# Attention layer 1 in two passes over its pairs of heads, with landmarks as means of projected tokens and pinv beside attn1

## The chip, the cores and the metric

The kernel runs on one core of a Trainium2 chip. The core has five engines that run beside each other and meet at semaphores: TensorE (PE in the profile, its weight loads PEld), VectorE (DVE), ScalarE (ACT), GpSimd (POOL) and SyncE (SP), which here issues most DMAs. Matmul results land in PSUM, [...]; everything else lives in SBUF or in DRAM. The metric is the device time of one launch in microseconds, the median of several runs.

## The reference

The input is `x` of 2 x 512 x 64 x 32, that is two batches of 2048 tokens with 512 channels, all in fp32. Layer 0 is full softmax attention with 8 heads of 64 and an embedding added to queries and keys, an output projection and a residual. Layer 1 is Nyström attention on the layer-normed tokens, and then a feed-forward map that is one 512 x 512 matrix (a 4-bit table product with `W`), each with a residual. In short:

```
q, k, v = split(ln(t) @ Wqkv);  q = q * scale
qL, kL  = means of q and k over groups of l = 8 tokens       # 256 landmarks
attn1   = softmax(q @ kL.T)       # 2048 x 256
attn2   = softmax(qL @ kL.T)      # 256 x 256
attn3   = softmax(qL @ k.T)       # 256 x 2048
out = attn1 @ (pinv(attn2) @ (attn3 @ v)) + conv33(v)
t = t + out @ Wout + bout;   t = t + ln(t) @ M
```

`pinv` is six steps of an iteration with 256 x 256 products. Its start is scaled by the largest row and column sums over all heads and both batches, so no head's pseudo-inverse can start before `attn2` of every head is there. Because a mean commutes with a projection, the landmarks can be had either by projecting means of tokens or by taking means of projected tokens.

## The kernel before, in words

Heads are worked in pairs: 64 + 64 channels fill the 128 partitions, and there are 4 pairs in each of 2 batches, numbered n = 0 to 7. Tokens are taken in four blocks of 512 (`TB`, `NTB`).

TensorE, VectorE, ScalarE and GpSimd execute in exactly the order in which the Python code emits their instructions; SP's DMAs are placed by the framework as soon as their buffers allow. So the code is a set of generators ("units") that yield after a piece of work, and the order of the calls decides what stands beside what. `advance(gens, n)` runs up to n units; a generator can yield `GAP` to let one call pass.

Layer 0: `attention0(hd, filler, ...)` runs one pair's attention, 64 steps of scores, exp and values, and between them units of the next pair's projections (`Heads0.units`) or of a batch's end (`finish0_units`, which calls `norm0_steps` for the layer norm of layer 1 and writes the normed tokens `xn` to DRAM as `xh`). `norm0_steps` also sums `xn` over groups of 8 tokens (L992), which gives the pooled tokens.

Layer 1, landmarks: `Landmarks.project` (L1178) multiplies the pooled tokens with the weights of q and k (`lp`, L1183), `attend` makes `attn2` (`X`), and `gram` makes its Gram matrix (`A`). `landmarks_beside(0)` does so for batch 0 beside the last attention of layer 0; `landmarks_staged(1)` (L1268) does so for batch 1 in a stretch of its own before the first pair. `X`, `A` and the landmarks `L` go to DRAM. Then `start_scale` makes the common scale.

Layer 1, pairs: the loop at L1850 does for each n, one after the other: `attn3` with the pair's `queries` (L1399, L1366); `landmarks_values` (attn3 @ v, normed, `Y`); `convolution` into the output tile `o`; `iteration_start` (L1476: load `A`, scale it into `M`, multiply `X` with `Y`); `pinv` (L1533: five iterations of squares `pa` and `pb`, each followed on VectorE by `less`, L1552, and on ScalarE by `flip`, which copies a transposed block; then three products `wp`, `tp`); the next pair's `keys`; and `attn1` with the next pair's `values`. `attn1` (L1614) keeps its scores in a tile of two PSUM banks with one exp over both, its values in a bank of its own, and the sums `rs` in a bank `pp`, where a reciprocal on VectorE (L1642) reads them.

PSUM is full: two banks `pp`, taken in turn by every `bank(...)`; two tiles `sc` of two banks each; and `av0`, `av1`, taken in turn by `values_bank`.

The end of a batch, `finish1_units` (L1716), is for each token block the output projection `yp` (four units), a layer norm (`mean`, squares, `var`), and the map `fp` (four units, each of which reads the `fp` of the unit before). Batch 0's end is filler: three units at each of the ten places of `pinv` for n = 4, and what is left is drained at n = 5, at the line

```python
            while hp == 1 and fill:
                advance(fill)
```

Batch 1's end comes last, with its own order (`turns`).

## Time and profile before

| | us |
|---|---|
| median of 3 runs (lowest, highest) | 2877.85 (2871.69, 2879.75) |
| the profiled execution's own time | 2879.97 |
| its span, first to last instruction | 2878.2 |
| TensorE busy with matmuls | 2787.5 |
| VectorE busy | 1746.6 |
| ScalarE busy | 870.6 |
| GpSimd busy | 262.5 |
| layer 0 up to its last attention | 0 to 1275 |
| that attention, with batch 0's landmarks | 1275 to 1464 |
| batch 1's norm beside pair 0 | 1464 to 1581 |
| batch 1's landmarks | 1581 to 1644 |
| the pairs of layer 1 | 1644 to 2750 |
| the end of batch 1 | 2750 to 2878 |

A row of the groups gives the line, the engine, the operation, what it writes and reads, how often, and then busy time in us, the mean of one in ns, and idle time before it with what ended it. A matmul of the code in fp32 shows as two rows of the trace. Matmuls overlap, so the busy time of a group is less than its count times its mean; the time from one start to the next is what counts. In a stage table each line is a stretch: its limits, its length, busy time (and number of instructions) of PE, PEld, DVE, ACT and POOL, the granted TensorE clock, the DMA share and GB/s.

### The profile page before, as it was taken

How to read it: one execution, taken by the hardware profiler on the slowest of the kernel's cores; microseconds unless marked ns; L12 is line 12 of the kernel's file. 1: busy time of each engine (PE TensorE's matmuls, PEld its weight loads, DVE VectorE, ACT ScalarE, POOL GpSimd, SP SyncE). 2: the span in 40 equal slices, each digit the busy share in tenths (PEclk: the TensorE clock that was granted, in tenths of full speed). 3: DMA queues.
4: the chain of work that ended last, by engine and by line, in shares of the span. 5: the costliest groups of instructions: out<-in, count | busy, mean ns of one | idle time of the engine just before them, and what ended most of it. 6: DMA issues, size and time to landing. Idle time of an engine off the chain costs nothing. (4 is left out here: it accounts for less than half of the span.)

```text
span 2878.2 us, 39302 instructions
## 1 busy us (share of the span) xinstructions
PE 2787.5 (97%) x16834; PEld 1384.1 (48%) x16834; DVE 1746.6 (61%) x1955; ACT 870.6 (30%) x1158; POOL 262.5 (9%) x160
## 2 busy tenths in 40 slices
PE   8999999999999999999999999999999988999999
PEld 4343443434343343344444756566656534565633
DVE  3869788765667857657558364535445544454475
ACT  1344434433243344444331221212121301222110
POOL 1101011010101100100002010101010100001010
PEclk9999999999999999999999999999999999999999
DMA  3000000101012100022024200002000010000021
GB/s 114 1 5 1 5 1 1 60 15 45 27 47 73 51 1 1 1 79 79 28 74 167 87 14 17 17 20 83 6 23 32 17 53 34 10 19 13 1 72 47
DMA packets 78152, 103.59 MB, mean 36 GB/s; under 512 B 8320, under 2 KB 48016, under 8 KB 77712
## 3 DMA queue, kind: packets, MB, share of 16 engines
q1 hardware_dynamic: 73472, 84.16, 9.1%
q0 software_dynamic: 4416, 16.79, 1.5%
q8 instruction: 134, 2.20, 0.3%
q14 instruction: 50, 0.41, 0.0%
q10 hardware_dynamic: 80, 0.03, 0.0%
HBM read 64.13 MB, written 36.84 MB: 35 GB/s over the span
## 5 line engine op out<-in xcount | busy, mean ns | idle before, releaser
L1060 DVE TENSOR_TENSOR acc_f<-acc_f,p_f 128x1024 f32<-128x1024 f32 x448 | 609.9, 1361 | 239.6 <-ACT p_f L1050 211.3
L1050 ACT ACTIVATE p_f<-sc_f 128x1024 f32<-128x1024 f32 x512 | 497.0, 1022 | 574.0 <-PE sc_f L1042 566.5
L1042 PE MATMUL sc_f<-q_f,k_f 64*64 64x512 f32 x4096 | 494.2, 598 | 3.3 <-ACT p_f L1050 3.3
L1072 PE MATMUL av_f<-p_f,v_f 64*64 64x512 f32 x4096 | 484.0, 589 | 0.0
L1072 PEld LDWEIGHTS av_f<-p_f,v_f 64*64 64x64 f32 x4096 | 156.6, 133 | 282.9 <-issue 282.9
L1042 PEld LDWEIGHTS sc_f<-q_f,k_f 64*64 64x64 f32 x4096 | 144.2, 133 | 292.0 <-issue 251.6
L1329 PE MATMUL pp<-xh,w 128*128 128x512 f32 x512 | 234.2, 603 | 5.8 <-ACT q L1335 2.3
L1540 PE MATMUL pa<-M 128*128 128x192 f32 (+1 forms) x640 | 156.9, 381 | 0.0
L1645 POOL TENSOR_TENSOR o<-o,rinv 128x512 f32<-128x512 f32 x32 | 58.3, 1821 | 1028.2 <-DVE rinv L1643 1025.5
L1540 PE MATMUL pb<-R 128*128 128x192 f32 (+1 forms) x640 | 151.2, 379 | 0.0
L1329 PEld LDWEIGHTS pp<-xh,w 128*128 128x128 f32 x512 | 93.5, 191 | 117.4 <-issue 102.4
L1091 POOL TENSOR_TENSOR q_f<-q_f,rinv_f 128x512 f32<-128x512 f32 x32 | 67.5, 2109 | 850.1 <-DVE rinv_f L1090 850.1
L1642 DVE RECIPROCAL rinv<-rs 128x512 f32<-128x512 f32 x32 | 107.4, 3356 | 56.2 <-PE rs L1638 56.2
L909 PEld LDWEIGHTS vp<-w,xh 128*128 128x128 f32 x1024 | 118.4, 194 | 25.8 <-ACT p L1610 14.6
L909 PE MATMUL vp<-w,xh 128*128 128x128 f32 x1024 | 124.0, 280 | 3.3 <-ACT R L1516 3.3
L1540 PEld LDWEIGHTS pb<-R 128*128 128x128 f32 x640 | 113.9, 193 | 25.5 <-issue 0.5
L1540 PEld LDWEIGHTS pa<-M 128*128 128x128 f32 x640 | 111.5, 196 | 25.0 <-issue 2.0
L909 PEld LDWEIGHTS vp_f<-wv_f,x 128*128 128x128 f32 x1024 | 115.6, 192 | 12.7 <-issue 10.2
L924 PE MATMUL yp_f<-q_f,wo_f 128*128 128x512 f32 x256 | 118.8, 619 | 2.4 <-DVE rinv_f L1090 2.4
L864 PE MATMUL pp_q_f<-x,wq_f 128*128 128x512 f32 x256 | 118.4, 616 | 1.1 <-DVE ft_q_f L850 0.7
L909 PE MATMUL vp_f<-wv_f,x 128*128 128x128 f32 x1024 | 118.5, 276 | 0.0
L924 PE MATMUL yp_g<-o,wo_f 128*128 128x512 f32 x256 | 113.4, 596 | 4.0 <-DVE xb_g L931 2.2
(193 smaller groups left out, 2973.6 us busy)
## 6 DMA issues: line engine op xcount, KB each, us to landing
x<-in_x_dram SPq DMA_DIRECT2D x8, 1024.0 KB, 5.3
xr_f<-in_x_dram SPq DMA_DIRECT2D x8, 1024.0 KB, 5.0
x_fd<-xr_f POOLq DMA_DIRECT2D x8, 1024.0 KB, 4.7
xh_fd<-xn_f POOLq DMA_DIRECT2D x8, 1024.0 KB, 4.6
xh<-xh_fd SPq DMA_DIRECT2D x8, 1024.0 KB, 5.0
xb_g<-x_fd SPq DMA_DIRECT2D x32, 256.0 KB, 4.6
out_dram<-xb_g SPq DMA_DIRECT2D x32, 256.0 KB, 2.3
w<-in_wqkv_dram SPq DMA_DIRECT2D x24, 256.0 KB, 3.7
```

What stands on the lines that cost most here:

```text
L864: nc.tensor.matmul(pp, lhsT=w_sb[kind][:, k, cols], rhs=xbs[t][:, k, :], start=k == 0, stop=k == KC - 1)
L909: nc.tensor.matmul(vp[:, j * P : (j + 1) * P], lhsT=xb[:, k, j * P : (j + 1) * P], rhs=w_of(k), start=k == 0, stop=k == KC - 1,)
L924: nc.tensor.matmul(yp, lhsT=wo_sb[:, k, m * P : (m + 1) * P], rhs=oTs[k][:, toks], start=k == 0, stop=k == NPAIR - 1,)
L1042: nc.tensor.matmul(sc[r * D : (r + 1) * D, h, :], lhsT=hd.k[rows, lo : lo + D], rhs=hd.q[rows, t * TB : (t + 1) * TB], start=True, stop=True,)
L1050: nc.scalar.activation(p, sc, AF.Exp, scale=D**-0.5)
L1060: nc.vector.tensor_tensor(acc, first if c == 1 else acc, p, ALU.add)
L1072: nc.tensor.matmul(av[r][half, :], lhsT=hd.v[keys, c, half], rhs=pp[keys, h, :], start=c == 0, stop=c == NST - 1,)
L1091: nc.gpsimd.tensor_tensor(o, o, rinv, ALU.mult)
L1329: nc.tensor.matmul(pp, lhsT=self.w[:, k, j, :], rhs=self.xhs[t][:, k, :], start=k == 0, stop=k == KC - 1)
L1540: nc.tensor.matmul(dst, lhsT=lhsT[:, k, t * P : (t + 1) * P], rhs=rhs[:, k, :], start=k == 0, stop=k == 1)
L1642: nc.vector.reciprocal(rinv, rs)
L1645: nc.gpsimd.tensor_tensor(o, o, rinv, ALU.add)
```

## The change

Layer 1 is cut into two passes over all eight pairs.

Pass 1 does for each pair the projections, the landmarks, `attn2` with its Gram matrix, `attn3`, the product of `X` with `Y` (now stored as `y0`), and the convolution. `Pair.front` yields how many units of another generator go after each piece, and `beside` puts the next pair's projections (`keys`, `queries`, `values`) there. The landmarks come from the projected keys and queries: `landmarks_of` sums 8 tokens at a time on VectorE. Pooled tokens, `Landmarks.project`, `landmarks_beside` and `landmarks_staged` are gone. Queries `q`, outputs of the convolution `o`, `y0`, `A` and `L` go to DRAM.

Pass 2 does for each pair `load` (all of these back, a pair ahead), `iteration_start` (the scaling alone) and `pinv(slot)`. A slot runs one unit of the attn1 of the pair before, and one unit of `fill`: the last pair's convolution at n = 0, batch 0's end from n = 5 on. There is a slot before `pinv`, two in each of its five iterations, one before the last flip and two in each of the three products, 18 in all. After the last pair, its attn1 and what is left of `fill` run by turns.

`attn1` now takes single `pp` banks for its scores, with one exp for each head, and does its blocks one after the other; `pinv`'s flips and transposes use the bank `av0` alone, attn1's values `av1`.

```diff
-    def norm0_steps(b, t, xb, xn, part, pooled=None):
+    def norm0_steps(b, t, xb, xn, part):
...
-        other = nc.vector if t == NTB - 1 else nc.gpsimd
-        other.tensor_tensor(xn[:, 2:, :], xn[:, 2:, :], wide, ALU.mult)
+        nc.gpsimd.tensor_tensor(xn[:, 2:, :], xn[:, 2:, :], wide, ALU.mult)
...
-        for to, of in parts:
-            nc.vector.tensor_reduce(to, of.rearrange("p k (m l) -> p k m l", l=POOL), AX.X, ALU.add)
...
+        def landmarks_of(self, j, src, scale):
+            L = self.L[:, j, :]
+            nc.vector.tensor_reduce(L, src.rearrange("p (m l) -> p m l", l=POOL), AX.X, ALU.add)
+            nc.vector.tensor_scalar(L, L, scale / POOL, None, ALU.mult)
+            self.largest(2 + j, L)
+            self.largest(j, src)
...
+        def front(self, then=lambda: None):
+            self.attend()
+            yield 2
+            for h in range(2):
+                self.gram(h)
+                yield 0
+            then()
+            for _ in self.attn3():
+                yield 1
+            for _ in self.landmarks_values():
+                yield 1
+            for _ in self.start_values():
+                yield 1
...
+        def load(self):
+            self.A = [zpool.tile([P, 2, LM + 1], F32, tag=f"Q{h}", name=f"A_{self.name}_{h}") for h in range(2)]
...
+                    nc.sync.dma_start(self.A[h][:, t, cols], A_d[self.b, self.hp, h][:, t, cols])
...
+            nc.sync.dma_start(self.q, q_d[self.b, self.hp])
...
+            nc.sync.dma_start(self.o, o_d[self.b, self.hp])
...
-                advance(gens, n_fill)
+                slot()
                 for h in range(2):
                     pr = square(R[h], f"pb_{it}_{h}_{self.name}", flip)
                     less_in_blocks(M[h], rest, M[h], pr)
                     flip = None
-                advance(gens, n_fill)
+                slot()
                 self.flip(M[0], f"M0_{it}")
...
-                    sc = scores_bank(f"sc1_{self.name}_{t}_{j}")
-                    for h in range(2):
+                    scs = [bank(f"sc1_{self.name}_{t}_{j}_{h}") for h in range(2)]
+                    for h, sc in enumerate(scs):
...
+                    for h, sc in enumerate(scs):
+                        nc.scalar.activation(p[:, h, :], sc, AF.Exp, scale=D**-0.5)
                     yield
...
+    rest = chain(next_keys, pairs[1].queries(), pairs[1].values())
+    conv = pairs[0].convolution()
     for n, (b, hp) in enumerate(todo):
+        pair = pairs[n]
         if n:
+            for _ in beside(pair.front(start_scale if n + 1 == len(todo) else lambda: None), rest):
+                pass
+        drain(rest)
+        if n + 1 < len(todo):
+            for _ in pair.convolution() if n else conv:
+                pass
...
+    pairs[0].load()
+    ones_before, fill = [], [pairs[-1].convolution()]
+    def slot():
+        advance(ones_before)
+        advance(fill)
...
+    for n, (b, hp) in enumerate(todo):
+        pair = pairs[n]
+        if not n:
+            advance(fill, 2)
+        advance(ones_before, 2)
+        pair.iteration_start()
+        if n + 1 < len(todo):
+            pairs[n + 1].load()
+        slot()
+        pair.pinv(slot)
+        while ones_before:
+            advance(ones_before)
+        ones_before.append(pair.attn1())
+        os.append(pair.o)
+        if hp == 0 and b:
+            fill.append(finish1_units(b - 1, os[:NPAIR]))
+            os = os[NPAIR:]
+    while ones_before or fill:
+        advance(ones_before)
+        advance(fill)
```

## The prediction

> **What bounds the kernel now.** I read the busy table first, then groups of instructions by shape, then the stages, then single timelines.
>
> ```profile
> PE 2787.5 (97%) x16834; PEld 1384.1 (48%) x16834; DVE 1746.6 (61%) x1955; ACT 870.6 (30%) x1158; POOL 262.5 (9%) x160
> ...
> L1183 PE MATMUL lp<-pooled,wL 128*128 128x256 f32 x128 | 31.0, 399 | 1.2 <-ACT X L1209 1.2
> L1642 DVE RECIPROCAL rinv<-rs 128x512 f32<-128x512 f32 x32 | 107.4, 3356 | 56.2 <-PE rs L1638 56.2
> ```
>
> TensorE bounds it: what it no longer does is saved, what makes it wait is lost. A full 512-column row costs 0.43 us in a stream (32 `yp_f` in 13.83 us at 1481.72), so a matmul in the code, which is two rows, costs 0.86. Next, busy time by stage (length, then PE, PEld, DVE, ACT, POOL, clock):
>
> ```profile
> 1581.00:1644.00 63.00, 58.08 (x286) 44.96 (x284) 23.31 (x52) 16.47 (x39) 3.65 (x9) 0.95 0.33 107
> 1842.70:1973.30 130.60, 128.99 (x722) 79.53 (x720) 63.42 (x99) 30.34 (x55) 11.98 (x8) 1.00 0.06 17
> 2334.60:2415.00 80.40, 61.03 (x128) 25.63 (x127) 37.06 (x38) 6.84 (x9) 0.00 (x0) 0.85 0.13 44
> 2722.70:2750.00 27.30, 24.39 (x114) 8.53 (x112) 18.18 (x18) 9.63 (x13) 4.22 (x2) 1.00 0.21 71
> ```
>
> In order: batch 1's landmarks; one whole pair (n=2), nearly full at full clock; the part of batch 0's end that runs alone; the last pair's attn1. The slack is in stages 1 and 3. The timelines show why pinv needs no filler and where two PSUM banks bind:
>
> ```profile
> 1893.10 0.81 PE L1540 MATMUL pb<-R 128*128 128x192 f32 x4
> ...
> 1895.29 0.75 DVE L1553 SCALAR_TENSOR_TENSOR M<-M,pb 128x320 f32<-128x320 f32 x2 [0.57 <-PE pb L1540]
> ...
> 1896.81 0.27 PE L1530 MATMUL tp_M<-ident,M 128*128 128x128 f32 x1
> ...
> 2347.87 1.12 PE L946 MATMUL mean_g<-xn_g,mean_w 128*128 128x512 f32 x2 [2.83 <-DVE xn_g L943]
> 2355.12 2.05 PE L959 MATMUL var_g<-sq_g,mean_w 128*128 128x512 f32 x2 [6.13 <-DVE sq_g L956]
> ...
> 2746.55 3.35 DVE L1642 RECIPROCAL rinv<-rs 128x512 f32<-128x512 f32 x1
> ...
> 2749.95 3.70 PE L924 MATMUL yp_g<-o,wo_f 128*128 128x512 f32 x8 [1.51 <-DVE rinv L1642]
> ```
>
> One pinv iteration is 7.7 us with TensorE full: VectorE finishes head 0's `M` at 1896.04 and its flip comes at 1896.81. The last line is a matmul waiting until a 3.35 us reciprocal lets go of one of the two `pp` banks.
>
> [...] stage 3 reads 76% busy, but its 128 rows at 0.43 us are 55 of 80.4 us. [...] granted clock 0.85 in stage 3, 0.95 in stage 1, 1.00 where there are no gaps. [...]
>
> **The change, part by part** (us against the profiled execution: 2879.97, span 2878.2, 1.8 around it; the median 2877.85 is 0.35 below that span).
>
> (A) The `lp` matmuls go for both batches: 128 rows, 31.0 busy: **-30**. In their place `landmarks_of` reduces projected tokens on VectorE: 16 reduces of 128x2048 at the 2.29 us of `big<-k`, about 37, which the pass-1 stages hide (VectorE works half of a pair's time). Pooling leaves: 12 reduces, 18.5. No other matmul is added or lost; transposes and flips keep their number (two flips move from `iteration_start` into `pinv`).
>
> (B) Batch 1's landmark stage: at stream pace its work is 46.3 of 63.0 (`lp` 13.8, scores 3.4, gram 10.5, `pp` 6.9, `vp` 10.8, `wp_y` 0.9, each rows by 0.43 per 512 columns), so 16.7 is waiting. Afterwards `attend` and `gram` of pairs 1 to 6 have the next pair's projections beside them. Pair 7 has none: exp 0.60 (the 128x512 row of `X<-sc`), reduce 0.68, reciprocal 0.17, multiply 0.69 leave about 2.8 open; reciprocal 1.76, multiply 0.42 and three copies to `y0`, 3.4; the reload of `A`, whose buffer is the `X` just used, 2.1 to land plus issue and scaling, 2.5; half clock, 2: about 11. **-6**.
>
> (C) Without pooling, batch 0's last norm in layer 0 loses a 2.28 reduce before a `mean` that waited 2.84, and some half clock: -4; batch 1's norm beside pass 1 likewise -4 (its waits from 1524 on). **-8**.
>
> (D) Batch 0's end: before, 80.4 less 55 is about 26 of waiting. Afterwards its 40 units go one to a slot through pinv of n=5 to 7, 56 calls for 54 slots. A slot runs one attn1 unit (scores, scores, values, `rs` in turn) and then one of these, so I wrote both sequences side by side. In three slots, an `rs` falls beside a map unit whose predecessor `fp` still holds the other bank: `fp` waits for VectorE's tail 1.65 (head 1's `less`, from 1893.10 to 1894.71) and the reciprocal 3.35, less its own 0.96: 4 each, 12. In seven, scores (now two single banks) wait until VectorE has passed `less` and read `fp`: 1.6 each, 11. Mean beside `rs` (subtract 2.29 behind the reciprocal), squares 2.3 on ACT ahead of a flip's copy, sqrt with table loads: 9. `xr` has one buffer: after the last store (2.3) and reload (4.6) VectorE stands with pinv's `less` behind it, three times 2.3: 7. Switches: 5. Sum 44. **+18**.
>
> (E) The last attn1 has no fill left. With two banks a block takes 8.4: `rs` 0.96, reciprocal to 4.45, second score half, two exps of 0.60 each, values 1.8, `acc` 1.22. Four blocks: 5.4 + 3x8.4 = 30.6, against 21.1 before (19.0 from 2730.96, and two score units earlier). **+9.5**.
>
> (F) attn1 in the slots of the next pinv. Queued behind each `rs` reciprocal on VectorE are pinv's `less`: 1893.10 shifted by `rs` makes VectorE free at +5.7, so head 0's `M` is 0.5 late for its flip: 0.65 with the switch, three times. Score units put 1.2 of exp ahead of the flip's copy: 0.5, three times. The 16 attn1 units last only to slot 13 of 0 to 17; at n=1 to 4 the last two products have nothing beside them: copy and transpose 0.65 twice, and the last `rs` reciprocal stands before `less`: 3.1. A switch to a group that waits costs 0.1 to 0.26 beside its pace in stage 2 (8 `pp` rows take 3.63 for 3.43, 32 `vp` 3.77 for 3.51). Per pair then, pass 1: projections 8x0.2, values 4x0.26, attn3 1.4, gram 0.6, convolution 0.7, the rest 0.7, together 6.0. Pass 2: pinv's own 1.85 as before, `rs` 1.95, the three score units 1.5, the other units 1.4, the first two score units 1.0 (their banks are waited for), products 5.3 (3.1, two times 0.65, switches), together 13.0. That is 19.0, against 11.3 in stage 2 (130.6 less its work at pace, 119.3) plus 1.5 for landmarks: +6.2 for n=1 to 4, 25; n=5 to 7 have fill there, +2.8, 8; [...]. **+40**.
>
> (G) `landmarks_of` in the last layer-0 attention, 5.2 of VectorE at its end ahead of the residual adds: +4; n=0 without fill in its products: +1. **+5**. Moved DMAs: each pair stores `q`, `o` (1 MB, about 5 us like `xh`), `y0`, `A` and `L` in pass 1 and loads them in pass 2, all on SP; `X`, `pooled` and the landmarks' weights leave it. The 32 large ones are 160 us of 1500 and I put them at 0: they are issued a pair ahead, hidden by a pair's 68 to 75 us of other work. Without that cover each would cost its 5.
>
> Sum: -30 - 6 - 8 + 18 + 9.5 + 40 + 5 = **+28.5**: span 2906.7, runs **2906**. Bounds of what the trace doesn't show: D's 44 from 15 (its 28 calls beside pinv n=4 lengthened that stage only from 130.6 to 132.0) to 60; F's 40 from 8 (switches alone) to 55; loads from 0 to 32.
>
> **Rivals.** *Covered waits* (faster): the slots hold enough TensorE work that reciprocals and bank holds stay hidden. For it: VectorE is busy only 61%, and n=4. Against: that stage had three units to a slot and attn1 kept its own two-bank scores. With D at 15 and F at 8: 28.5 - 29 - 32 = -32.5, so 2845. It decides when D and F together add under 29.5 instead of 58.
>
> *Level*: half of those waits arise: 2877.
>
> *Late loads*: SP takes its DMAs in order; the load of `L` for n+1 waits for the last scores of n-1 and `q`, `o`, `xr` could stand behind it. For it: `xb_g` already shows 12.0 us of DMA waits. Against: they are needed a pair later. At 4 us for each of eight pairs: 2938.
>
> **How the numbers follow.** 0.60 for the forecast (2888 to 2936), 0.20 covered (2825 to 2868), 0.12 level (2869 to 2887), 0.08 late loads (2936 to 2960). A change under 0.3% can't be told from none. Faster 0.20, same 0.12, slower 0.68. Leaving out the lower half of the covered case and the late loads: 2848 to 2938.
>
> **What would show it.** Right: no `lp`; no stage at clock 0.85 in the middle; second-pass stages longer than work at pace, with `sc`, `fp` and `wp` waiting for VectorE `rinv`, `y` and `less`; an attn1 tail near 30 us. Wrong: pinv stretches at 7.7 us an iteration plus the units' pace (F and D hidden), or TensorE waiting for DMA of `A`, `q` or `o`.

## The result, and the profile after

| | before | after |
|---|---|---|
| median (lowest to highest), us | 2874.77 (2871.60 to 2879.75) | 2939.2 (2936.78 to 2943.92) |
| ratio, 95% interval | | 1.0225 [1.0202, 1.0247] |
| profiled span, us | 2878.2 | 2938.2 |
| mean granted TensorE clock | 0.989 | 0.981 |

The change makes the kernel 2.2% slower. The forecast was 2906, so its direction was right and its size too small: +28.5 forecast, +60.0 between the two profiled spans.

The busy table of the kernel after, and its row of attn1's reciprocals (line, engine, operation, count, busy time, mean ns, idle time before and its releaser):

```profile
PE 2813.9 (96%) x16706; PEld 1374.2 (47%) x16706; DVE 1771.2 (60%) x2005; ACT 878.2 (30%) x1218; POOL 220.0 (7%) x130
...
L1582 DVE RECIPROCAL rinv<-rs 128x512 f32<-128x512 f32 x32 | 107.3, 3353 | 9.7 <-PE rs L1578 9.6
```

TensorE has 128 instructions fewer, the `lp` matmuls, and is "busy" 26 us longer. The second fact is no added work: a matmul at half clock lasts longer and counts as busy (below, four `sc` take 2.08 us, and 1.13 to 1.20 at full clock); whether that is all of the 26 us was not separated. The reciprocals are as many and as long as before; VectorE waited 56.2 us for the sums ahead of them then and 9.6 now. It has become the side that is waited for.

Busy time by stage of the kernel after (limits, length, then PE, PEld, DVE, ACT, POOL, clock, DMA share, GB/s):

```profile
1440.40:1587.90 147.50, 136.31 (x694) 81.92 (x692) 84.62 (x74) 38.49 (x50) 20.07 (x18) 0.97 0.32 113
1587.90:1659.40 71.50, 71.04 (x454) 46.25 (x452) 28.64 (x33) 18.31 (x29) 0.20 (x2) 1.00 0.16 55
...
2017.30:2054.70 37.40, 28.39 (x200) 19.42 (x199) 17.62 (x30) 12.71 (x20) 0.38 (x1) 0.90 0.48 151
...
2179.60:2255.30 75.70, 70.80 (x294) 39.56 (x294) 44.44 (x84) 15.01 (x41) 5.09 (x4) 0.93 0.07 23
...
2406.00:2777.00 371.00, 337.88 (x1148) 167.92 (x1148) 204.03 (x328) 69.74 (x149) 15.58 (x12) 0.95 0.06 22
2777.00:2813.00 36.00, 31.69 (x89) 9.58 (x89) 21.14 (x14) 8.04 (x14) 3.80 (x3) 0.91 0.16 52
```

In order: batch 1's norm with pair 0's front; one pair of pass 1 (n=1); the boundary from the last front to the first pinv; one pair of pass 2 (n=2); n=5 to 7 with batch 0's end; the last attn1. A pair took 130.6 before and takes 71.5 + 75.7 = 147.2 now. Pass 1 is full at full clock. Everything else on this list runs below it.

To say where time is lost I take, here and below, *waiting* as the time from one matmul's start to the next one's, less the matmul's pace (0.43 us for 512 columns and 128 x 128 weights, smaller ones in proportion). Half clock counts as waiting in this measure. Summed by stage, with what the steps had forecast (the row of A is not waiting but the 128 rows at their pace):

| stage (step) | forecast | measured |
|---|---|---|
| `lp` gone (A) | -30 | -27.5 |
| layer 0 up to its last attention (C) | -4 | -10.2 |
| the last attention, other than moved work | 0 | -6.7 |
| its first output block (G) | +4 | +7.8 |
| batch 1's norm and pair 0's front (C) | -4 | +4.4 |
| boundary of the passes (B) | -6 | -0.9 |
| pair n=0 (G) | +1 | +3.0 |
| pairs n=1 to 4, half clock included (F) | +32 | +49.0 |
| n=5 to 7, batch 0's end, last attn1 (D, E, F) | +36 | +42.5 |
| sum | +29 | +61.4 |

The spans differ by 60.0, so the rows together are 1.4 too high; a row depends on where a stage is cut and is good to about 2 us.

What TensorE waits for, longest sums first, from the view of waits of the kernel after (engine, what it would run, releaser: us in total, times, longest):

```profile
PE sc L1558 <- ACT p L1563: 15.0, 24, 1.1
PE tp L1475 <- ACT R L1470: 12.7, 14, 6.0
PE wp L1466 <- DVE R L1504: 11.5, 7, 2.6
PE fp_g L1638 <- DVE rinv L1582: 11.0, 3, 3.8
PE fp_q_f L853 <- DMA emb_f<-in_time_dram: 8.6, 1, 8.6
...
PE yp_f L929 <- DVE rinv_f L1078: 7.8, 2, 5.4
...
PE pa L1491 <- DVE M L1459: 2.9, 1, 2.9
```

The first three hardly show before the change (`wp` waited 1.6 for VectorE's `R` there). They are attn1's scores waiting for an exp to leave a `pp` bank, the products' transposes, and the products waiting for VectorE. The fourth is step D's three waits. The fifth, at the kernel's start, is the only direct wait for a DMA and was there before (8.5). Of the reloads one reaches TensorE, by way of VectorE: at the first pinv VectorE waits 3.82 for `y0` of pair 0 to come back (and 5.29 for `A`, while TensorE still runs the convolution), and the first squares wait 2.9 behind it (the last line). From then on no reload of `q`, `o`, `y0`, `A` or `L` is waited for.

The place that is dearest, from the timeline of the kernel after at the end of pinv for n=1, where the slots have run out:

```profile
2172.02 3.36 DVE L1582 RECIPROCAL rinv<-rs 128x512 f32<-128x512 f32 x1 [0.60 <-PE rs L1578]
...
2173.29 0.44 PE L1475 MATMUL tp<-ident,R 128*128 128x128 f32 x2 [0.53 <-ACT R L1470]
...
2176.02 0.48 DVE L1504 SCALAR_TENSOR_TENSOR R<-M,tp 128x128 f32<-128x128 f32 x2
2176.35 2.08 PE L1466 MATMUL wp<-M,R 128*64 128x256 f32 x8 [2.62 <-DVE R L1504]
...
2179.57 2.08 PE L1558 MATMUL sc<-q,L 64*128 64x512 f32 x4
...
2182.33 2.56 PE L1558 MATMUL sc<-q,L 64*128 64x512 f32 x4 [0.68 <-ACT p L1563]
```

The last reciprocal of pair 0's attn1 stands on VectorE ahead of the product step `R` of pair 1, so `wp` comes 2.62 late. At 2176.7 the clock halves for 10.24 us, and the eight `wp` and the first four `sc` of the next attn1 take 2.08 each where at full clock eight `wp` take 1.03 (at 2171.73) and four `sc` 1.13 to 1.20 (at 2202.47 and 2196.63). This repeats with every pair (2251.8, 2326.9, 2401.9).

### The profile page after: what moved, and what is told of

The parts are those of the page before. It is cut to its first block, busy times and chain, and to the rows that moved or that the text cites. A ratio compares the mean times of both kernels' runs of the same rounds, so it can differ in the third digit from the quotient of the medians.

```text
span 2938.2 us, 38995 instructions
## 1 busy us (share of the span) xinstructions
PE 2813.9 (96%) x16706; PEld 1374.2 (47%) x16706; DVE 1771.2 (60%) x2005; ACT 878.2 (30%) x1218; POOL 220.0 (7%) x130
## 5 line engine op out<-in xcount | busy, mean ns | idle before, releaser
L1491 PEld LDWEIGHTS pb<-R 128*128 128x128 f32 x640 | 109.8, 190 | 44.9 <-DVE R L1504 17.3
L1563 ACT ACTIVATE p<-sc 128x512 f32<-128x512 f32 x128 | 71.1, 595 | 175.0 <-PE sc L1558 160.7
L1504 DVE SCALAR_TENSOR_TENSOR R<-M,pa 128x320 f32<-128x320 f32 (+1 forms) x160 | 60.2, 418 | 103.9 <-PE pa L1491 103.9
```

The lines of the kernel that those rows point to most:

```text
L1491: nc.tensor.matmul(dst, lhsT=lhsT[:, k, t * P : (t + 1) * P], rhs=rhs[:, k, :], start=k == 0, stop=k == 1)
L1504: nc.vector.scalar_tensor_tensor(out, m, scale, pr, ALU.mult, ALU.subtract)
L1563: nc.scalar.activation(p[:, h, :], sc, AF.Exp, scale=D**-0.5)
```

## The experiments

All ratios are to the kernel before, measured in the same session. The waiting of one pair of pass 2 is that of n=2, from pinv's first square to the next pair's.

| kernel | median us | ratio, 95% interval | pair, us | waiting in it |
|---|---|---|---|---|
| after | 2939.2 | 1.0225 [1.0202, 1.0247] | 75.4 | 18.0 |
| e1_spread | 2931.02 | 1.0188 [1.0171, 1.0205] | 74.1 | 16.6 |
| e2_sums_copied | 2931.87 | 1.0198 [1.0181, 1.0215] | 77.2 | 19.8 |
| e3_last_two_banks | 2935.99 | 1.0207 [1.0190, 1.0224] | 75.7 | 18.2 |
| e5_clock_kept | 2928.36 | 1.0179 [1.0162, 1.0196] | 72.8 | 12.0 |
| e6_end_alone | 2966.64 | 1.0313 [1.0295, 1.0330] | 75.5 | 18.1 |
| e7_front0_beside | 2932.72 | 1.0193 [1.0176, 1.0210] | 76.6 | 19.1 |
| e8_own_attn1 | 2900.62 | 1.0084 [1.0067, 1.0100] | 74.8 | 17.3 |
| e9_start_first | 2893.2 | 1.0060 [1.0043, 1.0076] | 74.6 | 17.2 |
| e11_neighbour | 2905.38 | 1.0105 [1.0088, 1.0122] | 77.7 | 9.9 |
| e10_best | 2865.53 | 0.9964 [0.9950, 0.9978] | 74.5 | 17.1 |
| e12_two_sums | 2862.19 | 0.9953 [0.9937, 0.9970] | 73.1 | 13.9 |
| e13_flip_bank | 2847.3 | 0.9898 [0.9881, 0.9914] | 71.2 | 13.7 |
| e14_scaled_early | 2854.4 | 0.9925 [0.9908, 0.9941] | 67.4 | 10.0 |
| e15_two_sums | 2858.39 | 0.9946 [0.9929, 0.9963] | 68.2 | 9.1 |
| e16_scaled_in_four | 2837.91 | 0.9871 [0.9855, 0.9888] | 67.5 | 10.0 |

### Is a removed TensorE row worth its pace? (step A)

This one is the kernel before, with a quarter of `lp` in `Landmarks.project`:

```diff
-                for k in range(KC):
+                for k in range(1):
...
```

> The kernel before, with one of the four matmuls over channels left in each landmark projection (three quarters of the lp work is left out, so the landmarks are not the reference's). If TensorE sets the end and removed matmuls are saved one for one: 96 of 128 rows of 0.22 to 0.24 us, 21 to 23 us less than before. If part of them covered other waits in batch 1's landmark stage (scores, exp, multiply): about 10 us beside the attention and 3 to 6 of the staged 10, so 13 to 17. If landmarks lie off the path: under 5.

2855.02 (2849.69 to 2857.23), ratio 0.9921 [0.9904, 0.9938]: 21 us for 96 rows of 0.216. Removed rows count one for one, so step A stands and its gain was lost elsewhere.

### Is it attn1's units at the wrong slots? (step F)

```diff
     def slot():
-        advance(ones_before)
+        if slot.at not in (10, 11, 16, 17):
+            advance(ones_before)
         advance(fill)
+        slot.at += 1
```

> The changed kernel, with attn1's sixteen units taken at other slots: none at 10, 11, 16 and 17, so that the products at slots 12 to 15 have units beside them; same work, same instructions. Waits-in-slots theory: in the changed kernel the products of n=1 to 4 lose about 10 us each (2.8 before a transpose whose less stands behind a reciprocal, 1.8, then 3.5 and 1.2 at half clock); about 8 of each go, so 25 to 40 us less than the changed kernel, a stage from one pair's first product to the next of about 67 instead of 75.5 us, and no half-clock window there. Switch theory (the second pass is long because many small groups alternate): the same number of switches, so within 5 us of the changed kernel.

A third of a per cent, far from the 25 to 40 of the first theory. The pair n=1 fell from 75.6 to 71.3, but n=2 and n=3 took 74.1 and 76.2 after 75.4 and 75.2. At n=2 the products' `wp` and transposes wait 4.0 less, and 2.6 of it is waited elsewhere, most of it at the last flip (`tp_M`), the rest at values and scores. Which slot a unit takes is at most a small part of the cause.

### Are the three map waits those of a bank under a reciprocal? (step D)

```diff
-                nc.vector.reciprocal(rinv, rs)
+                nc.scalar.copy(rinv, rs)
+                nc.vector.reciprocal(rinv, rinv)
```

> The changed kernel, with attn1's sums copied by ScalarE from their PSUM bank to SBUF before the reciprocal, so the bank is free after 0.6 us instead of 3.4. Bank theory: the three waits of fp for the reciprocal (11.0 us together) fall to under 1 us each, with the half-clock windows behind them, and the last attn1 loses its wait for the bank (2.7 us in each of three blocks): 15 to 25 us less. Queue theory (the reciprocal hurts because pinv's less stands behind it on VectorE, whatever the bank): the fp waits stay near 3 us, the time falls by under 5 us or rises a little for the added copies.

The view of waits of this kernel, to be laid beside that of the kernel after:

```profile
PE wp L1466 <- DVE R L1504: 14.0, 7, 3.2
...
PE fp_g L1639 <- ACT rinv L1582: 2.1, 3, 0.7
```

The kernel won 7, where the bank theory had 15 to 25. The map's waits fell from 11.0 to 2.1: they were the bank, as step D had said. The pairs with batch 0's end beside them gave 2.4 and 3.5 back (n=5: 116.8 to 114.4, n=6: 114.7 to 111.2). But the pairs without it lost 0.4 to 1.8 each (n=2: 75.4 to 77.2): VectorE's queue is no shorter, and `wp` waits 14.0 instead of 11.5. Bank holds are a part of the loss and not its core.

### The last attn1 (step E)

```diff
-                    scs = [bank(f"sc1_{self.name}_{t}_{j}_{h}") for h in range(2)]
+                    both_banks = scores_bank(f"sc1_{self.name}_{t}_{j}") if wide else None
...
+                    if wide:
+                        nc.scalar.activation(p, both_banks, AF.Exp, scale=D**-0.5)
...
-        ones_before.append(pair.attn1())
+        ones_before.append(pair.attn1(n + 1 == len(todo)))
```

> The changed kernel, with the scores of the last pair's attn1 alone in the two-bank tiles, one exp over both, as in the kernel before; pinv no longer needs these tiles then. If the tail is long because of the two single banks: a block falls from about 9 to about 5.5 us, 10 to 14 us less in all. If it is bound by its chain of exp, values, sums and reciprocal whatever the banks: under 4 us.

It won 3 at most. The timeline of this kernel shows what a block waits for once its scores have banks of their own:

```profile
2786.10 3.36 DVE L1587 RECIPROCAL rinv<-rs 128x512 f32<-128x512 f32 x1 [1.32 <-PE rs L1583]
...
2789.49 0.69 DVE L1588 TENSOR_TENSOR rinv<-av,rinv 128x512 f32<-128x512 f32 x1
...
2790.33 3.27 PE L1576 MATMUL av<-p,u 128*64 128x512 f32 x8 [2.36 <-DVE rinv L1588]
```

Values may not start before the multiply behind the last block's reciprocal has read `av`, because attn1 has one values bank now and had two. The size in step E was near (8.4 a block, and 9.1 after), its reason, the two score banks, was one of several. In e8 below, with two-bank scores, both values banks and the blocks pipelined, a block takes 4.65, as in the kernel before; which of these does how much was not separated.

### Batch 0's end in the slots or alone? (step D)

```diff
-            fill.append(finish1_units(b - 1, os[:NPAIR]))
+            drain(finish1_units(b - 1, os[:NPAIR]))
```

> Edit: batch 0's end is run alone, at the place where it is handed to the slots (after pinv of n=4), so that pinv of n=5 to 7 has attn1 alone beside it. Theory end in slots is dear (step D: three waits of 4 for the banks of rs, 11 of score waits, 7 for the reload and more, 44 in all against 26 alone): 10 to 20 faster, 2919 to 2929. Rival (the end also fills the products of n=5 to 7, whose waits of 10 a pair come back without it, and alone it waits 26 and drops the clock): 5 to 25 slower, 2944 to 2964.

27 slower, more than the rival's upper end: alone the end takes 172 us at a clock of 0.86 (2405 to 2577), about 55 of it waiting where the theory had counted 26, and the pairs without it still wait 18 each. Putting the end into the slots, waits and all, is worth 27 us against running it alone in this order. A better order was not tried: batch 1's end has as many matmuls and takes about 127 us (2811 to 2938) in its own order and with more buffers. If there were room for that in the middle of the layer, the end alone would be some 45 us shorter, an estimate from the difference of the two, and the answer would turn round.

### The half clock

```diff
     def slot():
-        advance(ones_before)
-        advance(fill)
+        made = advance(ones_before) + advance(fill)
+        if not made and slot.pair:
+            idle = bank(f"idle_{slot.pair}_{slot.at}")
+            nc.tensor.matmul(idle, lhsT=halves, rhs=mT[:, 0, :], start=True, stop=True)
```

> Edit: at n=1 to 4, each slot that has no unit left gets one 128x512 fp32 matmul whose result nobody reads. Theory clock (each pair's half clock of 10.2 us after the sparse products costs about 4 us of the 17.4 waited per pair, and goes when TensorE has work in the gaps): the granted clock of the four pair stages goes from 0.93 to 0.98 or more and the kernel is 6 to 16 faster, 2923 to 2933, although it computes more. Rival (the half clock stands in time that waits for VectorE anyway, so its absence brings nothing and the added matmuls cost up to their 0.86 each): 0 to 12 slower, 2939 to 2951.

The stage of n=2 in this kernel, in the columns of the stage table:

```profile
2183.70:2256.50 72.80, 70.31 (x301) 39.57 (x301) 44.41 (x84) 15.01 (x41) 5.09 (x4) 1.00 0.07 24
```

VectorE's work is the same to 0.03 us, TensorE has 3.4 more of it, the clock is 1.00, and the pair is 2.6 shorter than after. The kernel won 11. So between 2.6 (what the pair got shorter) and 6.0 (if the added work filled no wait that would have been there at full clock too) of the 18.0 waited per pair came with the half clock. The remaining 12.0 are waits for VectorE, ScalarE and banks.

### Is it that attn1 sits in another pair's pinv at all?

attn1 goes back to the form of the kernel before: after its own pinv, with two-bank scores, three score units between the products, and its blocks pipelined. The slots keep only `fill`, and batch 0's end starts one pair earlier, beside n=4:

```diff
     def slot():
-        advance(ones_before)
-        advance(fill)
+        advance(fill, 2)
...
             self.product_transposed(wide, src, M, f"{i}")
-            slot()
+            next(self.scores)
-            tp = self.into_rows(wide, side_bank(0, f"tp_{i}_{self.name}"))
+            tp = self.into_rows(wide, values_bank(f"tp_{i}_{self.name}"))
...
         pair.pinv(slot)
-        while ones_before:
-            advance(ones_before)
-        ones_before.append(pair.attn1())
+        pair.attn1(fill)
```

> Edit: the changed kernel, with attn1 of the second pass in the form of the kernel before: directly after its own pinv, scores in tiles of two banks with one exp, three score units between wp and tp of the products, blocks pipelined, values in turn in both values banks. pinv's slots hold fill alone (the last convolution at n=0, then batch 0's end, two units a slot from n=4 on). Theory shared slots (what the change lost in the second pass comes from attn1 sitting in the slots of another pair's pinv, with single banks, and from batch 0's end sharing them, not from the lack of projections there): the pair stage of n=1 to 4 falls from 75.5 to 66 to 69 us, the stretch n=5 to 7 with the tail by about 45, in all 75 to 105 faster than the changed kernel, 2834 to 2865. Rival missing neighbour (pinv's products and attn1 wait as much once no projections stand beside them, wherever attn1 is): within 25 of the changed kernel, 2914 to 2960, pair stage 73 or more.

Neither theory holds whole. The kernel won 38, nearly all of it from n=4 on, where batch 0's end and the last attn1 are (how much of that is the end's earlier start was not separated), but the pair of pass 2 stayed at 74.8 with 17.3 waited. Its waits had only come together in one place, as the view of waits of this kernel shows:

```profile
PE tp_M L1481 <- DVE M L1455: 32.9, 5, 6.6
```

And the timeline of this kernel at one change-over, from attn1 of n=1 to pinv of n=2:

```profile
2197.20 3.35 DVE L1597 RECIPROCAL rinv<-rs 128x512 f32<-128x512 f32 x1
...
2200.59 0.69 DVE L1598 TENSOR_TENSOR rinv<-av,rinv 128x512 f32<-128x512 f32 x1
2201.19 1.55 DVE L1455 TENSOR_SCALAR M<-A,zs 128x256 f32<-128x256 f32 x2
...
2201.68 0.45 PE L1481 MATMUL tp_M<-ident,M 128*128 128x128 f32 x1 [6.58 <-DVE M L1455]
```

The next pair's scaling stands behind attn1's last reciprocal, and TensorE is empty for 6.58. That looked like an order to mend. The edit also brings the flips and the products' transposes back to the one bank `av0`, where e8 took the two values banks in turn, and gives batch 0's end one unit a slot:

```diff
                 if t:
                     values(t - 1)
                     advance(gens)
-                    sums(t - 1)
+                    if t == NTB - 1:
+                        before_last()          # iteration_start of the next pair
+                    if t < NTB or not late:
+                        sums(t - 1)
+            yield
+            if late:                           # in the next pinv's first slot
+                sums(NTB - 1)
+                yield
```

> Edit: as e8_own_attn1, but the scaling that starts the next pair stands on VectorE ahead of the last two reciprocals of attn1, the last block's rs, reciprocal and multiply go into the next pinv's first slot, flips and products' transposes keep one values bank, and batch 0's end takes one unit a slot and one a block of attn1 instead of two a slot. In e8 the pairs' change-over still cost 6.8 of waiting (VectorE scaled the next pair's A and y0 only behind the last reciprocal of 3.4) and 1.7 of half clock behind it, six times. Theory order (the second pass needs no projections beside it, only VectorE's work in an order that keeps reciprocals off the way): 35 to 50 faster than e8, 2850 to 2866, the pair stage of n=1 to 3 66 to 69 instead of 74.8, no half clock in it. Rival missing neighbour (with that wait gone the next one, in pinv's first squares and the products, takes most of its place): 2880 to 2900, pair stage 71 or more.

The kernel won 7 by the medians, and the pair stayed at 74.6, within what the rival, the missing neighbour, had forecast. The wait has another end now: the first flip waits for the multiply behind the reciprocal of block 2, which reads its values from the flips' bank. So a part of this wait was brought in by the edit itself; e13 below measures it. The view of waits of this kernel:

```profile
PE tp_M L1481 <- DVE rinv L1598: 21.0, 5, 5.5
```

The timeline of this kernel at the same change-over:

```profile
2200.60 1.55 DVE L1455 TENSOR_SCALAR M<-A,zs 128x256 f32<-128x256 f32 x2
...
2202.92 3.35 DVE L1597 RECIPROCAL rinv<-rs 128x512 f32<-128x512 f32 x1
2206.30 0.69 DVE L1598 TENSOR_TENSOR rinv<-av,rinv 128x512 f32<-128x512 f32 x1
...
2207.14 0.45 PE L1481 MATMUL tp_M<-ident,M 128*128 128x128 f32 x1 [5.51 <-DVE rinv L1598]
```

### What is missing beside attn1

A block of attn1 is 4.3 us of TensorE (scores 1.72, values 1.72, sums 0.86) and 5.3 of VectorE (add 1.22, reciprocal 3.36, multiply 0.69). Run by itself it leaves TensorE short. In the kernel before, the next pair's values projection stood in it: 128 rows at 0.108, 13.8 us that need VectorE for next to nothing (the expectation below has 10.8, too little). There TensorE waits only 2.9 us in the 31.3 from the scores of attn1 for n=2 to those of the next pair (1942.0 to 1973.3). The test puts back three quarters of that work, and nobody uses it:

```diff
                     values(t - 1)
-                    advance(gens)
+                    if not advance(gens) and self.b == 0 and self.hp:
+                        idle = bank(f"idle_{self.name}_{t}")
+                        for k in range(3):
+                            nc.tensor.matmul(idle, lhsT=halves, rhs=mT[:, k, :], start=k == 0, stop=k == 2)
```

> Edit: as e9_start_first, and at n=1 to 3 each block of attn1 has three 128x512 fp32 matmuls beside it whose result nobody reads: 2.6 a block, 10.3 a pair, about the 10.8 of the values projection that stood there in the kernel before. Theory missing neighbour (attn1 alone gives VectorE 5.3 a block, acc 1.22, reciprocal 3.36 and multiply 0.69, for 4.3 of TensorE, so TensorE waits 8 to 9 a pair at the change-over, 5.7 of it and the half clock behind; independent TensorE work there is nearly free): the pair stage grows from 74.4 to at most 77 and its half clock goes; the kernel is 0 to 8 slower than e9. Rival (the waits are those of the chain of the next pinv and stay): the pair stage grows by 8 or more, the kernel by 25 to 31.

The stage of n=2 of this kernel:

```profile
2206.00:2283.70 77.70, 75.00 (x318) 41.54 (x317) 45.99 (x84) 14.92 (x33) 6.75 (x5) 1.00 0.07 23
```

10.3 of added matmul work lengthened this pair by 3.1; waiting fell from 17.2 to 9.9, the wait at its change-over is gone, and the clock is 1.00. The pair n=1 grew by 4.9, and n=3, where a unit of batch 0's end already filled the change-over, by 6.4. The kernel is 12 slower than e9, a little beyond the theory's 8 and far from the rival's 25. So 4 to 7 of the 10.3 us were free in e9's form, which has the bank wait in it. That about as much was free in the kernel before, and that pass 1, where TensorE is busy for 71.0 of 71.5 us, now pays for it, is inferred and not tested.

### What exactly the change-over waits for

Four kernels on top of e10_best (below). e12_two_sums takes VectorE's add away for two blocks:

```diff
-                accs[t] = apool.tile([P, 2, 512], F32, tag="acc", name=f"acc1_{self.name}_{t}")
-                nc.vector.tensor_tensor(accs[t], *self.p1[t], ALU.add)
+                accs[t] = self.p1[t]           # rs from both tiles, accumulated
+                if t < 2:
+                    acc = apool.tile([P, 2, 512], F32, tag="acc", name=f"acc1_{self.name}_{t}")
+                    nc.vector.tensor_tensor(acc, *self.p1[t], ALU.add)
+                    accs[t] = [acc]
```

> Edit: as e10_best, and attn1's last two blocks take their sums rs on TensorE from both tiles of exps (two accumulated matmuls more for each block) instead of adding the tiles on VectorE first. It adds 0.86 of TensorE to each of two blocks and takes 1.22 of VectorE from each. By the missing neighbour theory TensorE waits for VectorE at the change-over 7 to 8 a pair, and VectorE's 2.4 less, with 1.7 more of TensorE's own time, cut the wait by 4.2 or more and the half clock behind it: 2.5 to 5 net a pair, 15 to 30 faster than e10, 2836 to 2850. Rival (VectorE isn't what the change-over waits for): 8 to 14 slower than e10, by the matmuls alone.

3 faster, which the intervals hardly tell from none, and not 15: the pair fell by 1.4, so VectorE's work alone is not it. e13_flip_bank moves the first two flips of a pinv from the bank that holds attn1's values to the `pp` banks; e14_scaled_early moves the scaling to GpSimd, two blocks earlier; e15_two_sums joins e14 and e12.

```diff
-            tp = side_bank(0, f"tp_{name}_{self.name}")
+            tp = bank(f"tp_{name}_{self.name}") if name in ("M0", "M1") else side_bank(0, f"tp_{name}_{self.name}")
...
-                    nc.vector.tensor_scalar(
+                    nc.gpsimd.tensor_scalar(
                         self.M[h][:, t, cols], self.A[h][:, t, cols], zs[:, 1:], None, ALU.mult
...
-                    if t == NTB - 1:
+                    if t == 1:
                         before_last()
```

> Edit: as e10_best, and the two flips that begin a pinv go to the two pp banks instead of the bank av0, which holds attn1's values of block 2 until the multiply behind its reciprocal. Theory bank (the change-over's 5.7 us end with that multiply because the flip waits for its bank): the wait falls by 2.5 to 3.5 at n=1 to 3 and the half clock behind it goes, 12 to 25 faster than e10, 2841 to 2854. Rival VectorE (pinv's first less is behind the same reciprocal anyway): the wait moves on to pinv's first squares, within 5 of e10.

> Edit: as e13_flip_bank, and the scaling of the next pair's A and y0 is done on GpSimd two blocks earlier instead of on VectorE ahead of the reciprocal of block 2. Theory VectorE (VectorE's 2.7 of scaling put off that reciprocal by as much, and pinv's first less stands behind it): 2 to 2.7 a pair faster than e13, 12 to 19 in all. Rival bank (the flips' bank was all of the wait): within 5 of e13.

> Edit: as e14_scaled_early, with the sums of the last two blocks taken from both tiles of exps as in e12_two_sums. Theory VectorE still ahead (pinv's first less waits for VectorE): up to 10 faster than e14. Rival (with the flips' bank and the scaling gone, VectorE is no longer late, and the added matmuls cost their 1.7 a pair): 5 to 14 slower than e14.

The bank is 3.4 of the wait at n=2 (17.1 to 13.7; 18 for the kernel, within the bank theory's 12 to 25), though n=3 did not get shorter (74.7 and 75.0). VectorE's scaling is another 3.7 (13.7 to 10.0), more than the 2.7 forecast; the clock of the stage, 0.98 in e13, is 1.00 in e16 below, where the scaling of this pair stands on GpSimd too. With both gone the two sums are no longer worth their matmuls (e15 is 4 slower than e14, the pair 0.8 longer). Yet e14 as a whole is slower than e13. It lost about 5 in the stage of n=4, and about 10 at its first pinv, seen in the timeline of this kernel:

```profile
2004.77 0.38 POOL L1158 PARTITION_ALL_REDUCE mall<-m  x1 [21.70 <-DVE m L1156]
...
2015.68 1.53 POOL L1467 TENSOR_SCALAR M<-A,zs 128x256 f32<-128x256 f32 x2 [10.54 <-issue]
2016.67 0.48 PE L1493 MATMUL tp_M<-ident,M 128*128 128x128 f32 x1 [9.45 <-POOL M L1467]
```

So the last kernel keeps GpSimd for the scalings of pairs 1 to 4 alone:

```diff
+            engine = nc.gpsimd if 1 <= self.i <= NPAIR else nc.vector
...
-                    if t == NTB - 1:
+                    if t == (1 if self.b == 0 else NTB - 1):
```

> Edit: as e14_scaled_early, but only the four scalings for pairs 1 to 4 are on GpSimd, two blocks early; the first one and those of pairs 5 to 7 stay as in e13_flip_bank. In e14 the pair stages of n=2 and 3 came out at 67.4 against 71.2 in e13, and it lost 10 at the first pinv, where GpSimd does the common scale's reduction right before, and 4 after n=4. Theory (VectorE's scaling ahead of the reciprocal is the rest of the change-over's wait): 9 to 15 faster than e13, 2832 to 2838. Rival (e14's short stages are paid for elsewhere, by loads or by GpSimd's sums into o): within 4 of e13.

2837.91, within the theory's range. Its stage of n=2, to be laid beside that of the kernel after:

```profile
2160.90:2228.40 67.50, 63.90 (x294) 37.53 (x294) 43.42 (x79) 14.93 (x33) 12.84 (x11) 1.00 0.08 26
```

The same 294 rows take 67.5 instead of 75.4. This kernel is 1.3% faster than the one before and 3.5% faster than the changed one. It still has the two passes, but attn1 follows its own pinv again; in the slots stand the last pair's front and convolution, batch 0's end and the sums of attn1's last block.

### The smaller stages (steps B, C, G)

```diff
-    more = [chain(pairs[0].values(), beside(pairs[0].front(), next_keys))]
+    rest = chain(next_keys, pairs[1].queries(), pairs[1].values())
+    more = [chain(pairs[0].values(), beside(pairs[0].front(), rest))]
```

> Edit: pair 0's front gets all projections of pair 1 beside it, where the changed kernel gives it only the keys. Theory tail (the 10 us that attn3's last values, rs and the transposes of pair 0 wait at 1536 to 1555 with nothing beside them, and the half clock behind them, are the part of step C that came out 8 worse than forecast): 7 to 12 faster, 2927 to 2932. Rival (the waits only move to pair 1's projections or to batch 1's norm): within 3 of the changed kernel, 2936 to 2942.

6.5 faster, 0.3%, at the edge of what can be told from none: just short of the theory's 7. e10_best has this edit, and two more on top of e9 (the last pair's `X` also gets another buffer, so that pair 0's `A` need not wait for it):

```diff
-    units = chain(gap(2), pairs[0].keys(), pairs[0].queries())
+    units = chain(gap(2), pairs[0].keys(), pairs[0].queries(True))   # query landmarks later
...
+    def values0():
+        for t, _ in enumerate(pairs[0].values()):
+            if t == 1:
+                pairs[0].query_landmarks()
+            yield
...
-            rest = iter(())
+            rest = pair.convolution() if n + 2 == len(todo) else iter(())   # beside front(7)
...
-    ones_before, fill = [], [pairs[-1].convolution()]
+    ones_before, fill = [], [chain(front, pairs[-1].convolution())]         # rest of front(7)
```

> Edit: as e9_start_first, and three more moves. Pair 0's front has all of pair 1's projections beside it (as e7, 6 to 7 there). The landmarks of pair 0's queries are summed after the first residual adds of batch 1's layer-0 end, not ahead of the last reciprocal of layer 0 (step G: the 7.8 wait of the first output projection and the half clock behind it). The last pair's attn2 and Gram matrix have the convolution of pair 6 beside them, and its attn3 and y0 go into the slots of the first pinv, before its own convolution. Theory: 6.5 + 6 to 8 + 8 to 12 = 20 to 27 faster than e9. Rival (each wait is replaced by another behind VectorE or the scores' banks): 8 or less faster than e9.

27.7 faster than e9 by the medians, in the same session, and above the theory's 27 by a little. The two profiled spans differ by 34.9, all of it by pair 1's pinv: 22 up to the sums of pair 1's attn3 (steps C and G), and 13 from there over the boundary (B).

The timeline of the kernel after shows the waits of pair 0's front, where TensorE had nothing beside attn3's end:

```profile
1538.56 2.27 DVE L1194 TENSOR_REDUCE big<-k 128x1 f32<-128x2048 f32 x1
1540.76 2.54 DVE L1329 TENSOR_TENSOR acc<-acc,p 128x1024 f32<-128x1024 f32 x2
1543.22 3.35 DVE L981 RECIPROCAL rstd_n<-rstd_n 128x512 f32<-128x512 f32 x1
...
1543.35 1.08 PE L1346 MATMUL rs<-acc,ones 128*64 128x256 f32 x8 [3.12 <-DVE acc L1329]
...
1550.01 0.69 PE L1360 MATMUL tp<-ident,acc 128*128 128x128 f32 x2 [5.57 <-DVE acc L1356]
```

It also shows G's wait, which e10 no longer has:

```profile
1418.75 2.28 DVE L1198 TENSOR_REDUCE L<-q 128x256 f32<-128x2048 f32 x1
...
1421.73 2.28 DVE L1194 TENSOR_REDUCE big<-q 128x1 f32<-128x2048 f32 x1
...
1424.12 3.36 DVE L1078 RECIPROCAL rinv_f<-rs_f 128x512 f32<-128x512 f32 x1
...
1427.53 13.05 PE L929 MATMUL yp_f<-q_f,wo_f 128*128 128x512 f32 x24 [5.40 <-DVE rinv_f L1078]
```

The landmarks of pair 0's queries, 5.4 of VectorE, stand ahead of the last reciprocal of layer 0, and three of the first four output projections wait for that.

## Why the prediction was right and wrong

**Direction.** Right, for the reason given: A's saving is real (one for one in e4), and D, E and F give back more. A took the 31.0 us for which the rows were busy, where B prices the same rows at 13.8 a batch; at their pace the 128 rows are 27.5. *Covered waits* falls; no stage of pass 2 came out hidden. *Late loads*, whose 2938 happens to be the measured time, falls too: it had 4 us for each of eight pairs, and though SP's queue stood at the loads of `L` (237.2 us in four waits), the one reload that TensorE felt, of `y0` at the first pinv, cost 2.9. A right number would have come from a wrong cause.

**The step that failed is F, in size, and it is the largest miss:** forecast +32 for n=1 to 4, of which 7 for the half clock were my own estimate with no trace behind it, measured +49. Pass 1 was right (6.0 forecast, 6.2 measured). Two terms were wrong. Pass 2 was put at 13.0, with that estimate 14.75, and took 17.4 on average over n=1 to 4. The term that was short is "products 5.3" and "the first two score units 1.0" with 1.75 of the estimate: 8.0, where 10.7 was measured, because F had 3.1 once, at full clock, while at n=2 the products' transposes wait 2.4, their `wp` 4.0, the next pair's first two score units 3.0 and the values behind them 1.3, most of it at half clock. The iterations themselves were no dearer than forecast. And F's base was 12.8 a pair where the pair before waited 11.3; the 1.5 for landmarks in it, which B had already counted for batch 1, make 6 over four pairs.

**The reason given in F is not the whole one.** F read the loss from attn1's units in the slots. With attn1 after its own pinv the pair waited as much (17.3, 17.2), so the slots are not needed for a loss of this size. A reading that fits the runs is this: what was taken away is the projection beside attn1, of which a good part was free there (e11); without it VectorE is the longer of the two engines in attn1, and its backlog reaches TensorE by whatever bank or operand comes next: `wp` and scores in the changed kernel, flips in e8 and e9. Once the flips' bank and the scaling were out of the backlog's way, 7 of the 17 were gone. All of that was measured with attn1 after its own pinv. For the changed kernel, where attn1 is spread over the slots, it is argued and not shown: e5 filled only the slots left empty, and no run put a neighbour beside its attn1 units.

**D** was right on the three `fp` waits (12 forecast, 11.0 measured, and e2 shows the bank). That the end would cost 18 more in the slots than where it was stands only as a part of the last row of the table (+36 forecast, +42.5 measured). Against running it alone in pass 2, in the order of e6, the slots save 27. **E** had a block's size within 0.7 and missed the values bank.

**C failed in sign for batch 1's norm** (-4 forecast, +4.4 measured). It counted the pooling that left, and A's sentence on `landmarks_of`, "which the pass-1 stages hide", was taken over unexamined: there VectorE holds the landmarks of the next pair's keys, 5.2 us, ahead of attn3's last adds, and a 3.35 norm reciprocal ahead of the division by its sums, and TensorE had nothing beside: its two waits are 3.12 and 5.57. Its first half came out better than forecast (-10.2 for -4); I did not test why. **B** put the boundary at 11, with an estimated 2 for the half clock, and it waits 16 at a mean clock of 0.90; it had a reload of `A` in it and none of `y0`, which is 2.9 of the rest. **G** is right in cause and half the size: 7.8 for 4, since the half clock came on top (the 24 rows of 0.43 behind the wait took 13.05 us, and the clock was 0.50 from 1427.5 to 1431.0).

**Slips in the sums,** none of them of weight: the tail that D reads off 1893.10 to 1894.71 is 1.61 and not 1.65, and F's 32 `vp` rows are 3.44 at pace and not 3.51.

**Open.** Pass 2 of e16 still waits 10 a pair without fill and 14 to 24 with batch 0's end; what the end's share is was not separated. Nor was the -6.7 in the last attention. Whether the end alone in a better order would beat the slots is open too.

## What to carry to other kernels

Before moving independent matmuls away from a stage, divide that stage's work by engine: where VectorE's part is longer (5.3 to 4.3 here), a good part of the matmuls beside it can be free (4 to 7 of 10.3 us in e11), and where TensorE is full they need not be (the 96 rows that e4 leaves out saved 21 us, their whole pace). Unused matmuls put into the stage measure that. When two dependent chains are put side by side, ask at the change-over which bank and which small operand of the next chain stand behind the last reciprocal of the one before; a spare bank and an operand made two blocks earlier were worth 7 us of 17 a pair. And a stage with short gaps can pay for them twice: the pair n=2, whose longest gap is 2.62 us, ran at half clock for 10.24 us of it, and with 3.4 us of unused work in the gaps it kept its clock and was 2.6 shorter.

## What the runs showed of the hardware

At 2176.7 in the kernel after, the clock halved with no idle gap over 2.62 us, the longest time from 2165 on in which TensorE ran no matmul; in the 3.41 us before the halving it ran matmuls for 0.76. The stretches at half clock in this kernel lasted 3.41, 6.83, 10.24 and 13.65 us; what sets these lengths was not shown. With 3.4 us of unused work in the gaps, the pair n=2 had no such stretch (clock 1.00, e5).

In e14 GpSimd ran its next tensor operation 9.9 us after the scale made from its all-reduce was ready (2005.8 to 2015.7), with nothing in the profile that it waited for. The kernel before has a pause of 6.8 us there (1628.5 to 1635.3), but its operand, too, was being reloaded then (issued from 1627.2 on). What makes either pause, no run here shows.
